# Graph network layer: sums of block pairs and of nodes turned by transposes instead of products with the identity

## The chip, the cores and the metric

The kernel runs on one core of a Trainium2 chip. Five engines of the core work on their own queues: TensorE (PE in the profile, its weight loads PEld), VectorE (DVE), ScalarE (ACT), GpSimd (POOL) and SyncE (SP, which here only issues transfers). The metric is the device time of one execution in microseconds. A kernel is timed in several runs and the median is taken. One further execution is recorded by the hardware profiler.

## The reference

A message-passing layer on a graph of 12,500 nodes and 400,000 edges, sorted by destination. Each node has 64 scalars and 32 vectors of three parts (160 numbers). Cut to its core:

```python
s, v = x[:, :64], x[:, 64:].reshape(n, 32, 3)
h_s = s @ lin1_ws * a / sqrt(64);  h_v = einsum('nci,cd->ndi', v, lin1_wv) * a / sqrt(32)
w1, w2, w3, w4, w5 = split(silu(edge_scalars @ fc_w1 / 8) @ fc_w2 / 8)   # 224 weights an edge
es, ev = h_s[src], h_v[src]                       # one row of 160 numbers for each edge
mid_s = concat(w1*es*e0, w4*einsum('eci,ei->ec', ev, e1)/sqrt(3))
mid_v = concat((w2*es)*e1, w3*ev*e0, w5*cross(ev, e1)/sqrt(2))
agg_s, agg_v = segment_sum(mid_s, dst)/4, segment_sum(mid_v, dst)/4
pre_s = sc_s + agg_s @ lin2_ws * a/sqrt(96);  pre_v = sc_v + einsum(agg_v, lin2_wv) * a/sqrt(128)
out = layernorm(x + concat(silu(pre_s[:, :64]), sigmoid(pre_s[:, 64:]) * pre_v))
```

All numbers are f32.

## The kernel before

**Tiles and blocks.** Edges go through in tiles of 128, one edge on each partition; 3,125 tiles. Three tiles are a block (1,042 blocks), and two blocks a pair (521 pairs), whose sums share one PSUM bank: one block on partitions 0 to 63, the other on 64 to 127. Since edges are sorted, the edges of a block reach few nodes; a window of `W` = 16 nodes from the block's first destination holds them (a loop at the end redoes the work if one does not). Four tiles are a step, and there are 782 steps.

**A step.** POOL issues four indirect transfers (`gather`, L471), each of which fetches 128 rows of `h_tab` into `hg`. TensorE makes the edges' 224 weights (`weights`, L546) from the hidden layer (`hidden`, L462, with ACT's activation L464) into `pw`. VectorE builds a one-hot of the destination within the window (L609), the products of weights and rows in `pr` (L556 and L564, 416 columns), and `sel` (L618), the one-hot times the four edge numbers. TensorE multiplies `sel` and `pr` into the bank `pa` (`add_tile`, L625): 64 rows for a block, which are four kinds (the scalar edge number and the three vector parts) times 16 nodes, and 416 columns.

**A pair's end.** When both blocks of a pair are summed, ACT copies `pa` to `sa` (`close`, L848). Some steps later `turned` brings channels onto the partitions: the 416 columns are taken as four groups of 128 (the last overlaps), and each is multiplied with those columns of the identity that hold the wanted kinds: the three vector kinds for groups 0 and 1, the scalar kind for groups 2 and 3. TensorE does this at L641, in the order of the pairs, and ACT copies the bank to `tt` (L644). There are 258 such calls for two pairs and five for one pair. When ten blocks are in `tt`, `second` multiplies them with the second weights (L654), ACT copies the result to `os` (L657), and VectorE adds each block's window to `acc` (`add`, L662).

**Nodes' ends.** When no open block can reach a group of 128-node tiles any more, `finish` turns their sums two tiles at a time: for each tile and each half (scalars, vectors) a product of the kept inputs with the `sc` weights (L709) and a product of `acc` with the identity (L711) are summed in one bank, `pp`. Then come the gates, the sum with `x` and the layer norm.

**The order.** All engines' orders are written out by hand (`manual_schedule`): every step puts its instructions on the queues in the order of the code. At step n TensorE gets weights(n), then at most a hidden layer, a turn or a second product (`spread_out`), and then the sums of step n-2. POOL's third gather of step n also waits for the weights of step n-2 (`behind`). `pw` has two buffers, `hg` five, `pr` and `sel` three. In every 66th step ACT's queue fetches the rows instead of POOL, one by one, spread over the steps before (L514).

Of the kernel before, what the change touches and what calls it, by code (L numbers as in the profile page):

```python
# [10 lines left out]
F32 = mybir.dt.float32  # L11
# [10 lines left out]
P = 128  # L22
S = 64
V = 32
V3 = 3 * V
# [6 lines left out]
W = 16  # L32
# [17 lines left out]
NPR = 2 * S + 3 * V3  # L50
ROWS = 4 * W
# [10 lines left out]
def gnn_kernel(  # L62
# [21 lines left out]
    nc = tc.nc  # L84
# [10 lines left out]
    consts = ctx.enter_context(tc.tile_pool(name="consts", bufs=1))  # L95
# [111 lines left out]

    ident = consts.tile([P, P], F32, name="ident")
    make_identity(nc, ident)
    iota_i = consts.tile([P, W], I32, name="iota_i")  # L210
    nc.gpsimd.iota(iota_i, pattern=[[1, W]], base=0, channel_multiplier=0)
    eps = consts.tile([P, 1], F32, name="eps")
# [19 lines left out]
    with tc.tile_pool(name="nodes", bufs=len(starts)) as nodes, tc.tile_pool(  # L232
        name="nodes_ps", bufs=6, space=PSUM
# [33 lines left out]
        for q in range(4):  # L267
            t0, s = divmod(q * QN, P)
            nc.gpsimd.dma_start(at_k[:P - s, q], attr[s:, t0:t0 + NQ])
            if s:  # L270
                m = min(NQ, NT - t0 - 1)
# [51 lines left out]
        for half in range(2):  # L323
            r = slice(half * S, (half + 1) * S)
# [14 lines left out]
        for c0, cn, xw, xz in loaded:  # L339
# [7 lines left out]
            n = min(cn, P)  # L347
# [7 lines left out]
            for u, c in enumerate(blocks):  # L355
# [8 lines left out]
                to = h_tab.rearrange("(q r) d -> r q d", q=4)[c0 + u * P:c0 + u * P + n]  # L364
# [39 lines left out]
    for to, part, pieces, w, r0, c0, by in maps:  # L404
        for k, piece in enumerate(pieces):
            four, at_p = divmod(PIECE[piece], 4)
            if four == 3:
                at_p = 3 - (len(PIECE) - 1) % 4 + at_p
            m = terms.setdefault((to, part, four), len(terms))
            at_r = at_p * V  # L410
            r = l2[at_r:at_r + V, m, c0:c0 + w.shape[1]]
# [16 lines left out]
    acc = sums.tile([V3, 2, NP], F32, name="acc")  # L428
# [199 lines left out]

    def turned(psum, sas, tt, b, n):

        pt = psum.tile([P, 8, 4, W], F32, name="pt", tag="misc")
        k = n * ROWS
        wanted = ident.rearrange("p (b k w) -> p k b w", b=2, k=4)[:k]
        for m, sa in enumerate(sas):
            plane = 0
            for four in range(4):
                c = min(four * P, NPR - P)
                of = slice(1, 4) if four < 2 else slice(0, 1)
                planes = slice(plane, plane + of.stop - of.start)
                plane = planes.stop  # L640
                nc.tensor.matmul(pt[:, planes, m * n:(m + 1) * n], sa[:k, c:c + P],  # L641
                                 wanted[:, of, :n], start=True, stop=True)
        n *= len(sas)
        nc.scalar.copy(tt[:, :, b:b + n], pt[:, :, :n])  # L644

    def second(pool, psum, tt, nb):
        po = psum.tile([V3, 2, NO, W], F32, name="po", tag="misc")
        for k, to in enumerate("sv"):
            of = [key for key in terms if key[0] == to]
            for n, (_, part, four) in enumerate(of):  # L650
                assert part and four < 2 or not part and four >= 2
                r = slice(P - V if four == 3 else 0, P)
                a = tt[r, four * 3 + part - 1 if part else 4 + four]
                nc.tensor.matmul(po[:, k, :nb], l2[r, terms[to, part, four]], a[:, :nb],  # L654
                                 start=(n == 0), stop=(n == len(of) - 1))
        os = pool.tile([V3, 2, NO, W], F32, name="os", bufs=1)
        nc.scalar.copy(os[:, :, :nb], po[:, :, :nb])  # L657
        return os
# [6 lines left out]
    def own_scalars_vectors(pool, c0, cn):  # L665

        xs = pool.tile([S, NF * P], F32, name="xs2")
        xv = pool.tile([V3, NF * P], F32, name="xv2")
        nc.sync.dma_start(xs[:, :cn], xs_t[:, c0:c0 + cn])
        nc.sync.dma_start(xv[:, :cn], xv_t[:, c0:c0 + cn])  # L670
        return xs, xv
# [8 lines left out]
    def finish(fin, psum, t0, nt, p, most=NF, pool=None):  # L680

        connect = pool is None and t0 + nt < tiles_of_nodes


        whole = nt if p == P else nt - 1
        xt = fin.tile([P, most, D], F32, name="xt") if pool is None else pool.tile([P, Q, D], F32, name="hg")
        if connect:
            xs, xv = own_scalars_vectors(fin, t0 * P, nt * P)
        held = []
        if whole < nt:  # L690
            nc.vector.memset(xt[:, whole], 0.0)
        parts = [(slice(t0 * P, (t0 + whole) * P), slice(0, whole), P)] if whole else []
        if whole < nt:
            parts.append((slice((t0 + whole) * P, (t0 + whole) * P + p), slice(whole, nt), p))
        for nodes_of, k, n in parts:
            nc.sync.dma_start(xt[:n, k], x[nodes_of, :].rearrange("(t p) d -> p t d", p=n))

        def turn(ks):
            if not held:
                held.extend(fin.tile([P, most, *shape], F32, name=name) for name, shape in (  # L700
                    ("g", [V3]), ("y", [D]), ("st", [6]), ("mv", [2]), ("rs", [])))
            g, y = held[:2]
            pp = psum.tile([P, 2, 2, V3], F32, name="pp", tag="misc")
            for k in ks:
                c = (t0 + k) * P
                for m in range(2):
                    if connect:
                        w, a = ((scs, xs), (scv, xv))[m]
                        nc.tensor.matmul(pp[:, k % 2, m], a[:, k * P:(k + 1) * P], w,  # L709
                                         start=True, stop=False)  # L710
                    nc.tensor.matmul(pp[:, k % 2, m], acc[:, m, c:c + P], ident[:V3, :V3],  # L711
                                     start=not connect, stop=True)
            for k in ks:
                nc.scalar.activation(g[:, k], pp[:, k % 2, 0], AF.Tanh, scale=half_at[:, t0 + k:t0 + k + 1])  # L714

            def gate():
                n = len(ks)
                k = slice(ks[0], ks[0] + n)
                nc.vector.scalar_tensor_tensor(y[:, k, :S], g[:, k, :S], 1.0, pp[:, :n, 0, :S],  # L719
                                               op0=OP.add, op1=OP.mult)  # L720
                for k in ks:
                    nc.vector.scalar_tensor_tensor(
                        y[:, k, S:].rearrange("p (c i) -> p i c", i=3),
                        g[:, k, None, S:].to_broadcast([P, 3, V]), 1.0,
                        pp[:, k % 2, 1].rearrange("p (i c) -> p i c", i=3),
                        op0=OP.add, op1=OP.mult)
                for k in ks:
                    nc.vector.scalar_tensor_tensor(y[:, k], y[:, k], half_at[:, t0 + k:t0 + k + 1],
                                                   xt[:, k], op0=OP.mult, op1=OP.add)

            return gate

        def moments():
            _, y, st, mv, _ = held
            for k in range(nt):
                nc.vector.bn_stats(st[:, k], y[:, k])
            for k in range(nt):
                nc.vector.bn_aggr(mv[:, k], st[:, k])

        def root():  # L740
            mv, rs = held[3:]
            nc.scalar.activation(rs[:, :nt], mv[:, :nt, 1], AF.Sqrt, bias=eps)

        def norm():
            _, y, _, mv, rs = held
            nc.vector.reciprocal(rs[:, :nt], rs[:, :nt])
            for k in range(nt):
                nc.vector.tensor_scalar(y[:, k], y[:, k], mv[:, k, 0:1], rs[:, k:k + 1],
                                        op0=OP.subtract, op1=OP.mult)
            for nodes_of, k, n in parts:  # L750
                nc.sync.dma_start(out[nodes_of, :].rearrange("(t p) d -> p t d", p=n), y[:n, k])

        return [lambda k=k: turn(range(k, min(nt, k + 2))) for k in range(0, nt, 2)] + [
            moments, root, norm]

# [9 lines left out]
    with tc.tile_pool(  # L765
        name="fin", bufs=1
    ) as fin, tc.tile_pool(
        name="mine", bufs=2
    ) as mine, tc.tile_pool(
        name="late", bufs=2  # L770
    ) as late, tc.tile_pool(name="edge", bufs=2) as edge, tc.tile_pool(
        name="deep", bufs=5
# [198 lines left out]
        with in_order:  # L971
# [74 lines left out]
            n = len(steps)  # L1046
# [29 lines left out]
        with tc.For_i(0, n_redo, 1):  # L1076
# [9 lines left out]
            with tc.For_i(0, n_again, 1) as g, tc.For_i(0, GT, 1) as k:  # L1086
# [7 lines left out]
                to = loads.tile([P, 1], I32, name="to1", bufs=1)  # L1094
# [15 lines left out]
                r = edge.tile([P, 1], F32, name="r", bufs=1)  # L1110
# [10 lines left out]
                with tc.For_i(first, last + 1, W) as base:  # L1121
# [5 lines left out]
                    sa = late.tile([P, NPR], F32, name="sa", bufs=3)  # L1127
                    nc.scalar.copy(sa[:ROWS], pa[:ROWS, :NPR])
                    tt = late.tile([P, 8, NO, W], F32, name="tt", bufs=1)
# [55 lines left out]
```

## Time and profile before

| | us |
|---|---|
| median of three runs | 4739.37 (4736.33 to 4754.99) |
| the profiled execution, its own time | 4726.69 |
| its span, first to last instruction | 4724.9 |
| busy in the span: PE / POOL / DVE / ACT | 4059.0 / 2944.0 / 2368.9 / 849.7 |

In rows of the profile, a group is a line, an engine, an operation, the tiles written and read, and a count; then busy time and the mean duration of one in ns, and the engine's idle time just before, with what ended it. In rows of equal stretches, a time stands for each engine (PE, PEld, DVE, ACT, POOL) with a count in brackets, then the clock granted to TensorE as a share of full speed, the transfers' share and GB/s. Durations of matmul passes overlap, so the pace of a group is read from one start to the next.

### The profile page before, as it was taken

Reading aid. Unit: us, or ns where it says so; the run is one execution under the profiler, and the core shown is the slowest. Engines: PE = TensorE matmul, PEld = TensorE weight load, DVE = VectorE, ACT = ScalarE, POOL = GpSimd, SP = SyncE. Lnnn points to the kernel's source line nnn. Section 1 sums busy time; section 2 is a strip of 40 time slices with the busy share of each in tenths; the row PEclk is TensorE's granted clock in tenths of the full one; section 3 lists DMA queues with packets and bytes.
Section 4 is the critical chain, followed back from the end, with each engine's and each line's share of the span. In section 5 each row is a group of like instructions: output and inputs, shape, how many; then the busy total and the mean of one; then the engine's idle time right before and its main releaser. Section 6 shows DMA issues by size and latency. Waiting matters only on the chain.

```text
span 4724.9 us, 69481 instructions
## 1 busy us (share of the span) xinstructions
PE 4059.0 (86%) x19977; PEld 2169.9 (46%) x19977; DVE 2368.9 (50%) x6421; ACT 849.7 (18%) x1828; POOL 2944.0 (62%) x3128
## 2 busy tenths in 40 slices
PE   6888888888888888888888888888888888888887
PEld 4444444444444444444444444444444444444444
DVE  5544544545544454455455445445445445544454
ACT  2111111111111111111121111111111111111112
POOL 6666666666666666666666666666666666666663
PEclk8888988988988889898998888888889888898898
DMA  6333333333333333333333333333333333333331
GB/s 212 87 77 79 91 86 79 91 78 86 94 77 86 78 94 86 77 94 83 80 93 85 84 89 87 84 86 79 91 88 79 91 81 87 91 80 88 78 92 50
DMA packets 253104, 413.30 MB, mean 87 GB/s; under 512 B 89304, under 2 KB 177153, under 8 KB 252581
## 3 DMA queue, kind: packets, MB, share of 16 engines
q0 software_dynamic: 150848, 263.03, 21.2%
q1 hardware_dynamic: 90004, 141.98, 12.6%
q10 hardware_dynamic: 11858, 3.76, 0.4%
q8 instruction: 159, 2.61, 0.2%
q14 instruction: 235, 1.93, 0.1%
HBM read 392.51 MB, written 16.00 MB: 86 GB/s over the span
## 4 chain that ended last, share of the span: by engine, by line
PE 52%; issue 15%; ACTq 9%; another core or an unknown queue 8%; DVE 8%; POOL 5%; DMA 2%; ACT 1%; DVEq 0%; SPq 0%; POOLq 0%
PE pa L625 18%; PE pw L546 12%; PE misc L641 8%; ACTq L514 7%; PE misc L462 6%; POOL hg L471 5%; PE misc L654 5%; DVE pr L564 4%; ACTq L507 2%; PE misc L711 1%; DMA hg<-h_tab,idx 1%; PE misc L709 1%; DVE sel L618 1%; DVE pr L556 1%
## 5 line engine op out<-in xcount | busy, mean ns | idle before, releaser
L471 POOL DMA_INDIRECT hg<-h_tab,idx x3081 | 2913.4, 946 | 1724.2 <-issue 792.5
L625 PE MATMUL pa<-pr,sel 128*64 128x416 f32 x6250 | 1564.8, 594 | 122.4 <-issue 120.5
L546 PE MATMUL pw<-w,hid 64*128 64x224 f32 x6250 | 988.1, 407 | 276.8 <-issue 178.9
L609 DVE TENSOR_TENSOR pw<-rel,iota 128x64 f32<-128x64 int16 x782 | 179.2, 229 | 1986.6 <-remote 1121.5
L564 DVE TENSOR_TENSOR pr<-pw,hg 128x384 f32<-128x384 f32 x2313 | 1137.6, 547 | 0.0
L546 PEld LDWEIGHTS pw<-w,hid 64*128 64x128 f32 x6250 | 626.1, 204 | 942.7 <-issue 653.7
L625 PEld LDWEIGHTS pa<-pr,sel 128*64 128x64 f32 x6250 | 445.8, 151 | 962.0 <-issue 921.4
L641 PE MATMUL misc<-ident,sa 128*128 128x96 f32 (+1 forms) x4168 | 600.2, 296 | 80.2 <-issue 76.9
L641 PEld LDWEIGHTS misc<-ident,sa 128*128 128x128 f32 x4168 | 559.2, 211 | 172.1 <-issue 154.5
L556 DVE TENSOR_TENSOR pr<-pw,hg 128x512 f32<-128x512 f32 x771 | 532.7, 691 | 38.5 <-DVE pw L609 5.1
L462 PE MATMUL misc<-es,w 128*128 128x512 f32 (+1 forms) x784 | 479.7, 695 | 43.4 <-DVE rel L424 20.0
L464 ACT ACTIVATE hid<-misc 128x512 f32<-128x512 f32 x392 | 233.1, 595 | 1092.7 <-issue 565.1
L644 ACT COPY tt<-misc 128x512 f32<-128x512 f32 (+1 forms) x263 | 152.8, 581 | 1434.0 <-remote 784.6
L654 PE MATMUL misc<-tt,l 128*96 128x256 f32 (+5 forms) x1496 | 371.8, 395 | 14.8 <-issue 14.2
L618 DVE TENSOR_TENSOR sel<-pw,eas 128x256 f32<-128x256 f32 x782 | 324.1, 415 | 0.1
L848 ACT COPY sa<-pa 128x416 f32<-128x416 f32 x521 | 262.2, 503 | 283.0 <-remote 83.8
L654 PEld LDWEIGHTS misc<-tt,l 128*96 128x96 f32 (+1 forms) x1496 | 232.0, 169 | 146.5 <-issue 81.2
L462 PEld LDWEIGHTS misc<-es,w 128*128 128x128 f32 x784 | 129.1, 205 | 174.1 <-issue 135.1
L662 DVE TENSOR_TENSOR acc<-acc,os 96x32 f32 x1042 | 192.1, 184 | 25.5 <-ACT os L657 7.0
L711 PE MATMUL misc<-ident,acc 96*128 96x96 f32 x392 | 115.0, 393 | 95.6 <-DVE acc L662 62.2
L719 DVE SCALAR_TENSOR_TENSOR y<-g,misc 128x128 f32<-128x128 f32 x49 | 14.1, 287 | 265.8 <-ACT g L714 75.4
L711 PEld LDWEIGHTS misc<-ident,acc 96*128 96x128 f32 x392 | 86.5, 276 | 112.3 <-DVE acc L662 66.9
(93 smaller groups left out, 726.2 us busy)
## 6 DMA issues: line engine op xcount, KB each, us to landing
es<-in_es_t_dram SPq DMA_DIRECT2D x258, 384.0 KB
hq<-h_tab ACTq DMA_DIRECT2D x5632, 0.6 KB
hg<-h_tab,idx POOLq DMA_INDIRECT x3081
h_tab<-ht POOLq DMA_DIRECT2D x24, 320.0 KB
xt<-in_x_dram SPq DMA_DIRECT2D x23, 320.0 KB
out_dram<-y SPq DMA_DIRECT2D x23, 320.0 KB
xv<-in_xv_t_dram SPq DMA_DIRECT2D x23, 192.0 KB
eat<-in_ea_dram SPq DMA_DIRECT2D x41, 96.0 KB
```

The costliest lines, as they stand in the source:

```text
L462: nc.tensor.matmul(ph[:k, c], w1[:k, :k], es[:k, t0 * P + c0 * P:t0 * P + c1 * P], start=True, stop=True)
L471: got = nc.gpsimd.indirect_dma_start(out=hg[:, t, :], out_offset=None, in_=h_tab, in_offset=bass.IndirectOffsetOnAxis(ap=i, axis=0))
L514: row = queue.dma_start(flat_hq[p:p + 1, t * row_bytes:(t + 1) * row_bytes], by_bytes[ds(v, row_bytes)][None])
L546: weighed.append(nc.tensor.matmul(pw[:, t, :NWT], hid[r, c * P:(c + 1) * P], w2[r], start=True, stop=True).ins.name)
L556: nc.vector.tensor_mul(two, pw[:, :n, :2 * S].rearrange("p t (k c) -> p t k c", k=2), hg[:, :n, None, :S].to_broadcast([P, n, 2, S]))
L564: nc.vector.tensor_mul(pr[:, :n, first:first + V3].rearrange("p t (i c) -> p t i c", i=3), pw[:, :n, None, 2 * S + k * V:2 * S + (k + 1) * ...
L618: nc.vector.tensor_mul(sel[:, :n], oh[:, :, None, :].to_broadcast([P, n, 4, W]), by_slot(tiles[0][0])[:, u:u + n, :, None].to_broadcast([P ...
L625: summed.append(nc.tensor.matmul(pa[half * ROWS:(half + 1) * ROWS, :NPR], sel[:, t].rearrange("p k w -> p (k w)"), pr, start=start, stop=s ...
L641: nc.tensor.matmul(pt[:, planes, m * n:(m + 1) * n], sa[:k, c:c + P], wanted[:, of, :n], start=True, stop=True)
L654: nc.tensor.matmul(po[:, k, :nb], l2[r, terms[to, part, four]], a[:, :nb], start=(n == 0), stop=(n == len(of) - 1))
L711: nc.tensor.matmul(pp[:, k % 2, m], acc[:, m, c:c + P], ident[:V3, :V3], start=not connect, stop=True)
L848: nc.scalar.copy(sa, pas.pop(j)[:, :NPR])
```

## The change

`turned` uses TensorE's transpose with a moving operand that is a permutation, instead of a product with some columns of the identity. A transpose has to write all four kinds (128 columns), so each also writes kinds that are not wanted, and the order of the writes is such that a later one overwrites them. Two permutations are used: the identity with its columns ordered by kind (`by_first`, scalar kind first) and a new constant, `first_last`, with the scalar kind last (`by_last`), which VectorE fills at the start. For two pairs, seven writes are transposes and one is still a product (the scalar kind of the second pair's third group, 32 columns). The second pair now comes first. The planes of `tt` stand in another order, so `second` reads others, and ACT's copy brings the pairs together. In `finish` the sums of nodes are turned by transposes as well, which start the bank; the product of the kept inputs follows and is added.

```diff
+    first_last = consts.tile([P, P], F32, name="first_last")
+    by_kind = ident.rearrange("p (b k w) -> p k b w", b=2, k=4)
+    ordered = first_last.rearrange("p (k b w) -> p k b w", b=2, k=4)
+    nc.vector.tensor_copy(ordered[:, :3], by_kind[:, 1:])
+    nc.vector.tensor_copy(ordered[:, 3:], by_kind[:, :1])
...
     def turned(psum, sas, tt, b, n):
-        pt = psum.tile([P, 8, 4, W], F32, name="pt", tag="misc")
-        k = n * ROWS
-        wanted = ident.rearrange("p (b k w) -> p k b w", b=2, k=4)[:k]
-        for m, sa in enumerate(sas):
-            plane = 0
-            for four in range(4):
-                c = min(four * P, NPR - P)
-                of = slice(1, 4) if four < 2 else slice(0, 1)
-                planes = slice(plane, plane + of.stop - of.start)
-                plane = planes.stop
-                nc.tensor.matmul(pt[:, planes, m * n:(m + 1) * n], sa[:k, c:c + P],
-                                 wanted[:, of, :n], start=True, stop=True)
-        n *= len(sas)
-        nc.scalar.copy(tt[:, :, b:b + n], pt[:, :, :n])
+        pt = psum.tile([P, 512], F32, name="pt", tag="misc")
+        k, w = n * ROWS, n * W
+        fours = {four: min(four * P, NPR - P) for four in range(4)}
+        by_first = ident.rearrange("p (b k w) -> p k b w", b=2, k=4)[:k, :, :n]
+        by_last = first_last.rearrange("p (k b w) -> p k b w", b=2, k=4)[:k, :, :n]
+        writes = [(0, 2, 0, by_first), (0, 3, 1, by_first), (0, 0, 2, by_last), (0, 1, 5, by_last)]
+        if len(sas) == 2:
+            writes = [(1, 1, 12, by_first), (1, 0, 9, by_first), (1, 3, 6, by_last), *writes,
+                      (1, 2, 8, by_first[:, :1])]
+        for m, four, at_p, moving in writes:
+            of = sas[m][:k, fours[four]:fours[four] + P]
+            kinds = moving.shape[1]
+            to = pt[:, at_p * w:(at_p + kinds) * w]
+            nc.tensor.matmul(to.rearrange("p (k b w) -> p k b w", k=kinds, b=n), of, moving,
+                             start=True, stop=True, is_transpose=kinds == 4)
+        m = len(sas)
+        nc.scalar.copy(
+            tt[:, :, b:b + n * m].rearrange("c f (m b) w -> c m f (b w)", m=m),
+            pt[:, :8 * w * m].rearrange("c (m f x) -> c m f x", m=m, f=8))
...
-                a = tt[r, four * 3 + part - 1 if part else 4 + four]
+                a = tt[r, 2 + four * 3 + part - 1 if part else four - 2]
...
                 for m in range(2):
+                    nc.tensor.matmul(pp[:, k % 2, m], acc[:, m, c:c + P], ident[:V3, :V3],
+                                     start=True, stop=not connect, is_transpose=True)
                     if connect:
                         w, a = ((scs, xs), (scv, xv))[m]
                         nc.tensor.matmul(pp[:, k % 2, m], a[:, k * P:(k + 1) * P], w,
-                                         start=True, stop=False)
-                    nc.tensor.matmul(pp[:, k % 2, m], acc[:, m, c:c + P], ident[:V3, :V3],
-                                     start=not connect, stop=True)
+                                         start=False, stop=True)
```

The first place is a call of `turned` for two pairs on TensorE, between the weights of one step and the sums two steps before it (`misc` is the bank it writes, `sa` the pairs' sums; a product stands here as one row, though the profile shows two passes of it). Before:

```order
L546 MATMUL pw_509<-w_92,hid 128x224 x4
L641 MATMUL misc_512<-ident,sa 128x3x32 x2
L641 MATMUL misc_512<-ident,sa 128x32 x2
L641 MATMUL misc_512<-ident,sa 128x3x32 x2
L641 MATMUL misc_512<-ident,sa 128x32 x2
L625 MATMUL pa_511<-pr,sel 64x416 x4
```

and with the change:

```order
L551 MATMUL pw_511<-w_95,hid 128x224 x4
L649 MATMUL misc_516<-ident,sa 128x128 x2
L649 MATMUL misc_516<-first_last,sa 128x128
L649 MATMUL misc_516<-ident,sa 128x128 x2
L649 MATMUL misc_516<-first_last,sa 128x128 x2
L649 MATMUL misc_516<-ident,sa 128x32
L630 MATMUL pa_514<-pr,sel 64x416 x4
```

There are still eight calls at the same place; seven of them stream 128 columns instead of 96 or 32, and the last is the product that is left.

The second place is one turn of two node tiles on TensorE, after the weights of a step (`acc` holds the nodes' sums, `scs` and `scv` are the weights of the kept inputs `xs` and `xv`). Before:

```order
L546 MATMUL pw_508<-w_92,hid 128x224 x4
L709 MATMUL misc_513<-scs,xs_1475 128x96
L711 MATMUL misc_513<-ident,acc 128x96
L709 MATMUL misc_513<-scv,xv_1476 128x96
L711 MATMUL misc_513<-ident,acc 128x96
```

and with the change:

```order
L551 MATMUL pw_511<-w_95,hid 128x224 x4
L717 MATMUL misc_516<-ident,acc 128x96
L721 MATMUL misc_516<-scs,xs_1478 128x96
L717 MATMUL misc_516<-ident,acc 128x96
L721 MATMUL misc_516<-scv,xv_1479 128x96
```

What reads `acc` now stands first, ahead of the product of the kept inputs.

## The prediction

> **What bounds the kernel now.** I read the page first, then the chain of waits, and then, because the two did not fit the gather engine's rows, POOL's own timeline and the busy time of equal stretches.
>
> ```profile
> PE 4059.0 (86%) x19977; PEld 2169.9 (46%) x19977; DVE 2368.9 (50%) x6421; ACT 849.7 (18%) x1828; POOL 2944.0 (62%) x3128
> PE 52%; issue 15%; ACTq 9%; another core or an unknown queue 8%; DVE 8%; POOL 5%; DMA 2%; ACT 1%; DVEq 0%; SPq 0%; POOLq 0%
> L471 POOL DMA_INDIRECT hg<-h_tab,idx x3081 | 2913.4, 946 | 1724.2 <-issue 792.5
> L556 DVE TENSOR_TENSOR pr<-pw,hg 128x512 f32<-128x512 f32 x771 | 532.7, 691 | 38.5 <-DVE pw L609 5.1
> L641 PE MATMUL misc<-ident,sa 128*128 128x96 f32 (+1 forms) x4168 | 600.2, 296 | 80.2 <-issue 76.9
> L711 PE MATMUL misc<-ident,acc 96*128 96x96 f32 x392 | 115.0, 393 | 95.6 <-DVE acc L662 62.2
> ```
>
> On these rows TensorE looks like the bound: busy 86%, half of the chain. POOL looks idle for a third of the time. Its timeline says otherwise:
>
> ```profile
> 2215.57 0.94 POOL L471 DMA_INDIRECT hg<-h_tab,idx  x1 [2.24 <-remote]
> 2216.82 0.94 POOL L471 DMA_INDIRECT hg<-h_tab,idx  x1 [0.30 <-issue]
> ...
> 2224.31 0.95 POOL L471 DMA_INDIRECT hg<-h_tab,idx  x1 [0.30 <-issue]
> 2227.51 0.95 POOL L471 DMA_INDIRECT hg<-h_tab,idx  x1 [2.25 <-PE pw L546]
> ```
>
> Gathers start every 1.25 us, eight in a burst, and then comes a pause of about 2.25 us. A burst with its pause takes 2227.51 - 2215.57 = 11.94 us, that is two steps. If TensorE set this length, it would follow TensorE's work. The next rows are such bursts, each from its first gather to the next burst's first; the bracket behind PE counts its matmul passes.
>
> ```profile
> 2215.57:2227.51 11.94, 9.94 (x37) 5.79 (x34) 3.53 (x9) 2.17 (x6) 7.56 (x8) 0.57 0.31 83
> 2239.64:2251.65 12.01, 10.90 (x63) 6.90 (x60) 6.59 (x17) 4.43 (x7) 7.56 (x8) 1.00 0.31 85
> 2263.77:2275.69 11.92, 8.74 (x46) 4.63 (x45) 5.78 (x16) 2.12 (x9) 7.57 (x9) 0.93 0.21 57
> 2275.69:2287.55 11.86, 11.86 (x49) 6.81 (x49) 5.78 (x16) 1.68 (x4) 7.53 (x8) 0.64 0.21 56
> 2299.39:2311.24 11.85, 9.81 (x47) 5.06 (x44) 5.58 (x15) 1.96 (x4) 7.58 (x9) 1.00 0.22 58
> 2371.37:2383.39 12.02, 10.57 (x64) 5.62 (x61) 6.86 (x24) 1.53 (x3) 7.60 (x9) 0.99 0.63 150
> ```
>
> From 37 to 64 passes, and with a granted clock (the number after POOL) from 0.57 to 1.00, the length stays between 11.85 and 12.02 us. The only thing that is the same in all of them is the eight gathers (a ninth is one that straddles an edge). So a gather with its share of the pause costs about 11.9/8 = 1.49 us, and this sets the pace. Over the whole run:
>
> ```profile
> 500.00:1000.00 500.00, 432.79 (x2119) 227.37 (x2118) 249.98 (x684) 89.40 (x195) 310.13 (x329) 0.89 0.34 85
> ...
> 4000.00:4500.00 500.00, 431.44 (x2147) 229.11 (x2149) 254.43 (x694) 87.77 (x194) 315.44 (x334) 0.90 0.34 85
> ```
>
> The eight stretches of 500 us from 500 to 4500 hold 329 to 336 gathers each, 2667 together: 1.50 us per gather. At 1.4875 they would take 3967 us. So only 33 us of 4000 (38 us over the run) are left for anything that stretches a burst, TensorE among it. What makes the pause I cannot name: of two equal pauses above the profile puts one down to an unknown releaser and one to the weights, pw.
>
> **The change, part by part.** *Turning the sums of block pairs.* A product of two f32 operands is two passes in the trace (521 pairs with four products each are the 4168 passes of L641). A call for two pairs is 16 passes:
>
> ```profile
> 2470.12 1.97 PE L641 MATMUL misc<-ident,sa 128*128 128x96 f32 x16
> 2472.03 1.62 PE L625 MATMUL pa<-pr,sel 128*64 128x416 f32 x8
> ```
>
> From start to next start that is 1.91 us, 0.119 us a pass. The new call has seven transposes and one product: nine passes, if a transpose is one. There is one transpose in the old kernel:
>
> ```profile
> 207.67 0.37 PE L791 MATMUL misc<-ident,far 128*1 128x128 f32 x1 [5.21 <-DVE far L788]
> 207.97 1.86 PE L546 MATMUL pw<-w,hid 64*128 64x224 f32 x8
> ```
>
> It is one record for one call, with 128 columns streamed as in the new calls; so the change does what it says. Its price beside neighbours is not shown. Below, the 0.119 us of the product passes, which load the same 128 columns of weights; above, the 0.30 us to the next start here, behind a wait and with one loaded column. I take 0.119, since the passes replaced have the same shape of load and stand in the same rows. With 258 calls for two pairs and five for one (258 x 16 + 5 x 8 = 4168) 4168 passes become 258 x 9 + 5 x 4 = 2342; 1826 x 0.119 = 217 us of TensorE time go. At the upper price a call takes 7 x 0.30 + 2 x 0.119 = 2.34 us, 0.43 us more than now, 111 us of TensorE time over 258 calls.
>
> The Trainium skill, TensorE: Matmul & The Clock Gate, Part 4 (PE-mode transpose), gives about 275 ns for a 128x128 transpose in one kernel's context; by it a call would take 7 x 0.275 + 0.24 = 2.16 us, and TensorE's time would grow by an estimated 65 us instead of shrinking by 217. The lone record here, 0.37 us with 0.30 us to the next start, is no evidence against that.
>
> *The order inside a call.* The second pair's sum now comes first. Before, a late second copy held up only the second half:
>
> ```profile
> 2062.31 0.19 PEld L641 LDWEIGHTS misc<-ident,sa 128*128 128x128 f32 x1 [0.32 <-issue]
> ...
> 2065.14 1.24 PEld L641 LDWEIGHTS misc<-ident,sa 128*128 128x128 f32 x8 [0.22 <-ACT sa L848]
> ```
>
> Here the whole call would wait until 2065.14, and behind it on TensorE the sums and the weights of the next steps, for which VectorE and the gathers wait. Few calls have this, so between nothing and the eight passes' 0.95 us per call; I take nothing, covered by the slack below.
>
> *Nodes' turns.* 392 passes of L711 become 196, and the product of kept inputs moves from ahead of the transpose to behind it:
>
> ```profile
> 2003.92 0.35 PE L709 MATMUL misc<-scs,xs 64*128 64x96 f32 x2
> 2007.81 0.74 PE L711 MATMUL misc<-ident,acc 96*128 96x96 f32 x2 [3.53 <-DVE pr L564]
> ...
> 2011.53 0.96 PE L625 MATMUL pa<-pr,sel 128*64 128x416 f32 x2
> ```
>
> Behind the wait stand 14 passes in 3.72 us, 0.27 us each; now there are 12, so 0.53 us less, and for the 47 turns that have this product 25 us of TensorE time.
>
> *The rest.* ACT's copy moves the same 512 elements. Two small copies at the start, under 0.7 us together by L556's 0.69 us for 512 columns, lie on VectorE ahead of the first work of the program; I count 0.3 us. The planes' new places change addresses alone.
>
> **The sum.** 242 us of TensorE time go, 0.62 us per two steps. Its cover is the pause of the bursts: the six rows above leave it idle 0 to 3.2 us in 11.9, and length does not follow passes, so within the steady bursts I count nothing. Where the cut is on the path:
>
> ```profile
> 4668.89 4.22 PE L641 MATMUL misc<-ident,sa 128*128 128x96 f32 x24
> 4673.04 1.86 PE L546 MATMUL pw<-w,hid 64*128 64x224 f32 x8
> ...
> 4707.83 3.73 PE L711 MATMUL misc<-ident,acc 96*128 96x96 f32 x16 [1.28 <-DVE acc L662]
> ...
> 4675.19 0.95 POOL L471 DMA_INDIRECT hg<-h_tab,idx  x1 [8.48 <-PE pw L546]
> ```
>
> At the end POOL waits 8.48 us for weights that stand behind 24 turning passes, and after the last gather TensorE is the chain. Eleven of these 24 go (11 x 0.176 = 1.9 us), 19 of the 40 after them (2.3 us), and eight of the last 16 (1.9 us): 6 us. Of the 38 us that stretch bursts I give the cut 14; bounds 0 and 38. Together 4726.7 (the profiled execution: span 4724.9 and 1.8 around it) - 20 = 4706.7. The median of the runs shown is 12.7 above it: 4719, rounded to 4718; by the bounds and the 6 us, 4695 to 4733, and its own range is 4690 to 4735.
>
> **Rivals.** *TensorE is the bound, as its 86% and the chain say.* Then up to 242 us come off: 4497; by the chain's 67% for PE and issue 162 us, 4577; middle 4540. Against it stand the rows from 37 to 64 passes. It would need the pause to be TensorE's lateness after all, shortened by being earlier.
>
> *Bursts grow longer.* A few bursts are of twelve:
>
> ```profile
> 2474.40:2491.92 17.52, 10.97 (x59) 5.52 (x57) 7.83 (x23) 2.42 (x8) 11.34 (x12) 0.82 0.22 59
> ```
>
> That is 1.46 us per gather, 0.03 less. If weights that are done earlier let most bursts run on, 3081 x 0.03 = 92 us come off: 4645. For it: the gather after the pause does wait for weights. Against: these weights wait for VectorE first, which is not changed.
>
> *Slower: the clock.* The granted clock falls after a stretch in which TensorE does little (the second and third row; the first is the mean of the run):
>
> ```profile
> core 0: 4724.9 us, clock 0.883
> ...
> 2003.90:2007.30 3.40, 0.37 (x4) 0.20 (x2) 2.51 (x6) 1.10 (x2) 1.89 (x2) 1.00 0.19 51
> 2007.30:2010.70 3.40, 2.89 (x11) 2.55 (x12) 1.25 (x5) 0.00 (x0) 2.60 (x3) 0.57 0.29 76
> ```
>
> If transposes do not count as work, each call is such a gap, and one beside another wait tips the clock. TensorE's 86% is 10.2 us of 11.9; less 0.62 it is 9.6 at the mean clock of 0.88 (first row). It fills the 11.9 us once the mean clock is under 0.88 x 9.6/11.9 = 0.71, and from there it sets the time: at 0.69 a burst takes 12.25 us, 0.35 x 391 = 137 us more, 4860; at 0.70 12.07 us, 66 us more, 4785. Against: a call of 1 us is a third of the 3.4 us nearly empty here, and the row of clock 0.57 above took 11.94 us too. The Trainium skill's Part 4 named above states that transposes do not count as busy in the same way; the one transpose of this trace cannot show it.
>
> **How the numbers follow.** Gathers set the time, small gain: 0.62. TensorE the bound: 0.14. Longer bursts: 0.09. Clock: 0.15. About 0.5% (24 us) is what a measurement of this kernel can tell from no change; of the first case I put 0.39 within it and 0.23 beyond. Faster is 0.23 + 0.14 + 0.09 = 0.46, same 0.39, slower 0.15. The range takes in the upper end of the TensorE case and the clock case down to a mean clock of 0.70: 4570 to 4780, which leaves out some 0.10 below and 0.08 above.
>
> **What would show it.** Right: the turning rows fall to 2342 passes, PE's busy share falls by four or five points, and the stretches still hold 329 to 336 gathers per 500 us with pauses near 2.2 us. A transpose's price: the time from a call's start to the next group, 1.07 us here, over 1.9 if it runs alone. Wrong: over 345 gathers per 500 us (TensorE was the bound, or bursts of twelve are common), or a mean clock under 0.71.

## The result and the profile after

| | before | changed |
|---|---|---|
| median of four runs, us | 4740.15 (4736.33 to 4754.99) | 4696.17 (4686.28 to 4703.92) |
| the profiled execution, us | 4726.69 | 4696.53 |

The ratio is 0.990, with a 95% interval from 0.9872 to 0.9929: 44 us faster, twice the 21 us that were forecast, on the side that was forecast and within the range.

From the changed kernel's page, the busy times, the chain of waits by engine, and the groups of the gathers, of the turning writes and of the nodes' transposes:

```profile
PE 3740.4 (80%) x17955; PEld 1866.6 (40%) x17955; DVE 2369.9 (50%) x6423; ACT 852.4 (18%) x1828; POOL 2943.9 (63%) x3128
PE 41%; DVE 15%; issue 15%; another core or an unknown queue 15%; POOL 7%; ACTq 5%; DMA 2%; ACT 1%; DVEq 0%; SPq 0%; POOLq 0%
L476 POOL DMA_INDIRECT hg<-h_tab,idx x3081 | 2913.4, 946 | 1695.3 <-issue 813.6
L649 PE MATMUL misc<-ident,sa 128*128 128x128 f32 (+1 forms) x1558 | 328.3, 301 | 230.7 <-issue 140.4
L649 PE MATMUL misc<-first_last,sa 128*128 128x128 f32 x784 | 199.3, 311 | 12.9 <-issue 12.6
L717 PE MATMUL misc<-ident,acc 96*128 96x96 f32 x196 | 68.0, 353 | 166.7 <-DVE pw L614 118.0
```

TensorE has 2022 passes fewer (19977 - 17955), as the change says: 1558 + 784 = 2342 turning passes are left of 4168, and 196 of the nodes' 392. Its busy time fell by 319 us and by six points of the span, the time of the program by 30 us (of these two executions). POOL's busy time is the same to 0.1 us, and its idle time ahead of gathers fell from 1724.2 to 1695.3 us: 28.9 us, nearly the whole difference. So what these two executions gained was gained in POOL's pauses. In the rows of equal stretches the same is seen as more gathers in 500 us (the number behind POOL):

```profile
500.00:1000.00 500.00, 404.77 (x1914) 196.78 (x1912) 252.81 (x692) 90.80 (x196) 314.09 (x333) 0.88 0.34 86
...
4000.00:4500.00 500.00, 403.80 (x1931) 199.46 (x1931) 252.96 (x692) 91.08 (x204) 315.57 (x334) 0.88 0.35 87
```

The eight stretches from 500 to 4500 hold 333 to 338 gathers (329 to 336 before), 2688 together instead of 2667. 21 gathers at 1.49 us are 31 us.

One call of the turning, with a granted clock of 1.00, from the timeline of TensorE (start, length, line, count):

```profile
4658.09 0.44 PE L649 MATMUL misc<-ident,sa 128*128 128x128 f32 x2
4658.36 0.27 PE L649 MATMUL misc<-first_last,sa 128*128 128x128 f32 x1
4658.47 0.38 PE L649 MATMUL misc<-ident,sa 128*128 128x128 f32 x2
4658.69 0.38 PE L649 MATMUL misc<-first_last,sa 128*128 128x128 f32 x2
4658.91 0.31 PE L649 MATMUL misc<-ident,sa 128*128 128x32 f32 x2
4659.15 1.03 PE L551 MATMUL pw<-w,hid 64*128 64x224 f32 x8
```

Nine passes in 4659.15 - 4658.09 = 1.06 us; 1.07 were forecast. The lone transpose of the second row lasts 0.27 us, and the next starts 0.11 us after it: one transpose is long, but here they follow each other at 0.11 us, close to the 0.119 us of the product passes that they replace. The prediction's upper price, 0.30 us from the one transpose of before, was read where the granted clock was 0.50.

### The profile page after: what moved, and what is told of

The parts are those of the page before. It is cut to its first block, busy times and chain, and to the rows that moved or that the text cites. A ratio compares the mean times of both kernels' runs of the same rounds, so it can differ in the third digit from the quotient of the medians.

```text
span 4694.7 us, 65476 instructions
## 1 busy us (share of the span) xinstructions
PE 3740.4 (80%) x17955; PEld 1866.6 (40%) x17955; DVE 2369.9 (50%) x6423; ACT 852.4 (18%) x1828; POOL 2943.9 (63%) x3128
## 3 DMA queue, kind: packets, MB, share of 16 engines
q0 software_dynamic: 150848, 263.03, 21.6%
q1 hardware_dynamic: 90004, 141.98, 12.7%
q8 instruction: 143, 2.34, 0.2%
## 4 chain that ended last, share of the span: by engine, by line
PE 41%; DVE 15%; issue 15%; another core or an unknown queue 15%; POOL 7%; ACTq 5%; DMA 2%; ACT 1%; DVEq 0%; SPq 0%; POOLq 0%
PE pa L630 14%; PE pw L551 10%; DVE pr L569 9%; POOL hg L476 7%; PE misc L664 5%; PE misc L467 4%; PE misc L649 4%; ACTq L519 4%; DVE sel L623 2%; PE misc L721 2%; DVE pr L561 2%; DMA hg<-h_tab,idx 1%; DVE pw L614 1%; PE misc L717 1%
## 5 line engine op out<-in xcount | busy, mean ns | idle before, releaser
L476 POOL DMA_INDIRECT hg<-h_tab,idx x3081 | 2913.4, 946 | 1695.3 <-issue 813.6
L630 PE MATMUL pa<-pr,sel 128*64 128x416 f32 x6250 | 1533.6, 590 | 96.8 <-issue 91.5
L551 PE MATMUL pw<-w,hid 64*128 64x224 f32 x6250 | 943.0, 398 | 318.5 <-issue 176.3
L551 PEld LDWEIGHTS pw<-w,hid 64*128 64x128 f32 x6250 | 601.8, 199 | 948.3 <-issue 600.9
L649 PE MATMUL misc<-ident,sa 128*128 128x128 f32 (+1 forms) x1558 | 328.3, 301 | 230.7 <-issue 140.4
L467 PE MATMUL misc<-es,w 128*128 128x512 f32 (+1 forms) x784 | 467.0, 674 | 52.4 <-issue 25.3
L664 PE MATMUL misc<-tt,l 128*96 128x256 f32 (+5 forms) x1496 | 391.3, 407 | 38.6 <-issue 35.2
L649 PEld LDWEIGHTS misc<-ident,sa 128*128 128x128 f32 x1558 | 231.6, 181 | 328.1 <-issue 217.2
L649 PE MATMUL misc<-first_last,sa 128*128 128x128 f32 x784 | 199.3, 311 | 12.9 <-issue 12.6
L717 PE MATMUL misc<-ident,acc 96*128 96x96 f32 x196 | 68.0, 353 | 166.7 <-DVE pw L614 118.0
L467 PEld LDWEIGHTS misc<-es,w 128*128 128x128 f32 x784 | 123.7, 196 | 181.5 <-issue 161.8
L649 PEld LDWEIGHTS misc<-first_last,sa 128*128 128x128 f32 x784 | 120.1, 162 | 16.4 <-issue 16.0
```

Of the source, the lines that this page charges most:

```text
L467: nc.tensor.matmul(ph[:k, c], w1[:k, :k], es[:k, t0 * P + c0 * P:t0 * P + c1 * P], start=True, stop=True)
L476: got = nc.gpsimd.indirect_dma_start(out=hg[:, t, :], out_offset=None, in_=h_tab, in_offset=bass.IndirectOffsetOnAxis(ap=i, axis=0))
L551: weighed.append(nc.tensor.matmul(pw[:, t, :NWT], hid[r, c * P:(c + 1) * P], w2[r], start=True, stop=True).ins.name)
L630: summed.append(nc.tensor.matmul(pa[half * ROWS:(half + 1) * ROWS, :NPR], sel[:, t].rearrange("p k w -> p (k w)"), pr, start=start, stop=s ...
L649: nc.tensor.matmul(to.rearrange("p (k b w) -> p k b w", k=kinds, b=n), of, moving, start=True, stop=True, is_transpose=kinds == 4)
```

## The experiments

The twelve runs were made on four chips, each beside the kernel before on the same chip. On the first three chips the kernel before takes 3956 us, not 4740, and in the traces from there gathers hardly ever pause; on the fourth, which had only the last run, it takes 4774 us. All expectations below were written with one of these two pictures in mind, and the ratio to the kernel before is what compares runs of different chips.

**The change again.** No edit.

> The changed kernel itself, beside the kernel before on the same chip. The four runs so far showed the kernel before at 3956.6 us instead of 4740, with gathers starting every 1.25 us without any pause. If this chip shows no pauses either: gathers set the time at 3081 x 1.25 = 3851 us plus start and end, so the change is worth only what lies after the last gather, 4 to 8 us, 3949 to 3953 us. If it shows pauses: 4690 to 4700 us beside 4740, 30 to 50 us less, as first measured.

Measured: 3950.24 us beside 3955.88, ratio 0.9985 (0.9975 to 0.9995). The timeline of POOL, here and in the first measurement of the changed kernel, shows what differs. First this run, 16 gathers in a row:

```profile
2207.34 0.95 POOL L476 DMA_INDIRECT hg<-h_tab,idx  x1 [0.30 <-issue]
...
2216.11 0.95 POOL L476 DMA_INDIRECT hg<-h_tab,idx  x1 [0.30 <-issue]
2217.36 0.95 POOL L476 DMA_INDIRECT hg<-h_tab,idx  x1 [0.30 <-issue]
...
2226.11 0.95 POOL L476 DMA_INDIRECT hg<-h_tab,idx  x1 [0.30 <-issue]
```

and then the first measurement:

```profile
2209.68 0.94 POOL L476 DMA_INDIRECT hg<-h_tab,idx  x1 [0.30 <-issue]
2213.00 0.94 POOL L476 DMA_INDIRECT hg<-h_tab,idx  x1 [2.38 <-PE pw L551]
...
2221.75 0.95 POOL L476 DMA_INDIRECT hg<-h_tab,idx  x1 [0.30 <-issue]
2224.79 0.94 POOL L476 DMA_INDIRECT hg<-h_tab,idx  x1 [2.09 <-PE pw L551]
```

A gather takes 0.95 us and starts 1.25 us after the one before in both. Only the pause of some 2.2 us after eight is missing here: a gather starts over 1.6 us after the one before it three times in this run and 413 times in the first measurement. Without pauses the program is the gathers' time, 3081 x 1.25 = 3851 us, with a start and an end, and 2022 passes less of TensorE are worth 6 us.

**One part alone.** The first run keeps the changed `turned` and has `finish` as before:

```diff
-                    nc.tensor.matmul(pp[:, k % 2, m], acc[:, m, c:c + P], ident[:V3, :V3],
-                                     start=True, stop=not connect, is_transpose=True)
                     if connect:
                         w, a = ((scs, xs), (scv, xv))[m]
                         nc.tensor.matmul(pp[:, k % 2, m], a[:, k * P:(k + 1) * P], w,
-                                         start=False, stop=True)
+                                         start=True, stop=False)
+                    nc.tensor.matmul(pp[:, k % 2, m], acc[:, m, c:c + P], ident[:V3, :V3],
+                                     start=not connect, stop=True)
```

The second is the kernel before with these lines the other way round, the transpose first.

> Only the turning of block pairs is changed; the nodes' turns are as before. It removes 1826 of the 2022 passes. Theory (gathers set the time, TensorE's cut shows only where a burst was stretched): the gain of the whole change, 44 us, splits about as the TensorE time does, so some 30 us of it come here, 4705 to 4715 us. Rival (TensorE sets the time): about two thirds of it too, but then the doubled writes of the fourth run must cost far more than 50 us.

> Only the nodes' turns are changed; block pairs are turned as before. It removes 196 passes and lets the reader of acc stand first. Theory: 10 to 20 us less than before, 4720 to 4730 us, since turns of nodes stand in stretched bursts (8 of the 26 worst of before). If the order mattered more than the passes, all 44 us could be here: 4696 us.

Measured: 0.9986 (0.9977 to 0.9995) and 1.0005 (0.9996 to 1.0014). Both figures in us were written for a chip with pauses and missed by the whole of its difference. The split itself is clear where there are no pauses: the block pairs bring all of the 6 us, the nodes nothing that can be told from zero. How the 44 us of the first measurement divide was not measured.

**The order of the two pairs.** The sums that were copied first are turned first:

```diff
-            turned(misc_ps, [sa for _, sa in js], tts[0], len(turns), 2)
-            for j, _ in js:
+            turned(misc_ps, [sa for _, sa in js[::-1]], tts[0], len(turns), 2)
+            for j, _ in js[::-1]:
```

> The whole change, but the pair whose sums were copied first is turned first. In the changed kernel turning waits 192 us in all for ACT's copy sa (89 before products, 103 before weight loads). Theory: three of nine writes run ahead of that wait, at most 0.33 us of 258 calls, 85 us of TensorE time, of which a tenth shows: 0 to 10 us less than the changed kernel, 4686 to 4696 us. Rival (TensorE sets the time): 40 us or more less.

Measured: 0.9987 (0.9978 to 0.9996), the change's own 0.9985 within the interval. The order is worth nothing here.

**Twice the work.** Every write of a call is issued twice:

```diff
-        for m, four, at_p, moving in writes:
+        for m, four, at_p, moving in [w for w in writes for _ in range(2)]:
```

> The whole change, and every write of a block pairs' call is issued twice in a row: 2342 more passes, about 0.115 us each, 270 us more work for TensorE. Theory (gathers set the time): the change took 378 us of TensorE's time away and gained 44, so 0.12 us per us: about 30 us more than the changed kernel, 4710 to 4740 us. Rival (TensorE sets the time): by the 56% that PE and issue have of the chain 150 us more, 4845 us; by its whole time 270 us, 4965 us.

The 378 us in this expectation stand in no page; the busy time fell by 319. Measured: 0.9996 (0.9987 to 1.0005). The same 500 us of the change and of the doubled writes, the first row the change's:

```profile
1000.00:1500.00 500.00, 434.62 (x2294) 219.84 (x2292) 300.63 (x826) 106.81 (x232) 378.08 (x401) 0.92 0.44 103
```

```profile
1000.00:1500.00 500.00, 460.27 (x2581) 252.05 (x2580) 301.50 (x827) 106.78 (x232) 377.80 (x399) 0.93 0.44 103
```

287 passes more in 500 us, 26 us more of TensorE's busy time, and two gathers fewer. Over the run 2342 passes cost 0.0011 x 3956 = 4 us. That is far under the 150 to 270 us of the theory that TensorE sets the time, which falls with this on a chip without pauses. It is also under the 30 us of the gathers' theory, which took its rate from the first measurement.

**The gathers' number.** With all rows of a kind fetched by POOL, 44 gathers more:

```diff
-OWN = 66
+OWN = 100000
```

> The changed kernel without steps whose rows ACT's queue fetches: POOL issues 44 more gathers, 3125 in all. Theory (gathers set the time): 44 x 1.25 = 55 us more than the changed kernel without pauses, 44 x 1.49 = 66 us more with them. Rival (TensorE or VectorE sets the time): no change, or a few us less since 5632 row transfers go.

Measured: 1.0113 (1.0096 to 1.013), 4000.69 us, 50 us over the change on the same chip: 1.15 us a gather. On this chip the gathers' number sets the time.

**The wait for the weights.** Without the wait of the third gather:

```diff
-                    deep, [index(t) for t, _, _ in tiles], {2: weighed_by[n - 2] if n >= 6 else None})
+                    deep, [index(t) for t, _, _ in tiles], None)
```

> The changed kernel without the wait of each step's third gather for the weights of two steps before; a gather then waits for its buffer alone. Theory (a gather takes 1.25 us of POOL whatever it waits for): no change without pauses, 3945 to 3960 us; with pauses no change either, if they come from buffers that are late, 4680 to 4710 us. Rival (the wait itself makes the pause): with pauses 4000 to 4400 us, from 3081 x 1.25 = 3851 us up to TensorE's time; without pauses no difference between the two.

Measured: 3947.07 us, 0.9977 (0.9967 to 0.9986). Without pauses the wait costs some 3 us, and the intervals of the two ratios overlap. Whether it makes the pauses on a chip that has them stays open: the run fell on a chip without.

**Gathers that wait for TensorE.** To make gathers wait for TensorE on a chip without pauses, the third gather waits for the weights of one step before instead of two, in both kernels:

```diff
-{2: weighed_by[n - 2] if n >= 6 else None}
+{2: weighed_by[n - 1] if n >= 6 else None}
```

> The kernel before, with the third gather of a step waiting for the weights of one step before instead of two. This makes gathers wait for TensorE, as they did in the first measurement, and is read together with the next run. Without pauses in the kernel before: bursts now end at a wait for weights, so slower than 3956 us, somewhere between 4050 and 4700 us. If weights are always long done when they are waited for: no change.

> The changed kernel with the same tighter wait. Theory (378 us of TensorE's time are worth little where gathers run back to back, and more where a gather waits for weights): the difference to the run with the kernel before is well over the 6 us found without pauses: 30 to 100 us less, as 44 us in the first measurement. Rival (the larger gain of the first measurement has nothing to do with the gathers' wait for weights): again 4 to 8 us less.

Measured on one chip: 4052.45 us, ratio 1.0252 (1.0235 to 1.0269), and with the change 4007.01 us, ratio 1.0126 (1.011 to 1.0143). The change is worth 45 us here, 1.1%, beside 6 us with the looser wait. POOL's waits for weights (total us, times, longest), first in the kernel before, then with the change, then in the change with the looser wait:

```profile
POOL hg L471 <- PE pw L546: 128.0, 87, 6.2
```

```profile
POOL hg L476 <- PE pw L551: 87.5, 79, 7.7
```

```profile
POOL hg L476 <- PE pw L551: 22.4, 48, 4.1
```

128.0 - 87.5 = 40 of the 45 us are this one wait. So the same cut of TensorE's work is worth some seven times as much where gathers wait for what TensorE makes, though the gathers set the pace in all three. It does not copy the first measurement: 60 pauses stand in the trace of the kernel before with the tighter wait, 442 in that of the first measurement.

**Fewer gathers, more of ACT's rows.** Every 44th step's rows are fetched by ACT's queue, three a slot:

```diff
-OWN = 66
-SLOTS = (2,2,2,2)
+OWN = 44
+SLOTS = (3,3,3,3)
```

> The changed kernel with every 44th step's rows fetched by ACT's queue instead of every 66th, three rows a slot instead of two: 17 such steps instead of 11, 24 gathers fewer. Theory (gathers set the time): 24 x 1.25 = 30 us less than the changed kernel without pauses, 24 x 1.49 = 36 us less with them. Rival: no change, or slower, if ACT with half as many transfers more becomes late with its copies.

Measured: 4159.62 us, 1.0478 (1.0407 to 1.0549). The rival came true. The chain of waits by engine of this run:

```profile
ACTq 52%; PE 16%; issue 12%; DVE 3%; ACT 2%; DMA 1%; POOL 1%; SPq 0%; DVEq 0%; POOLq 0%
ACTq L519 40%; ACTq L512 12%; PE pa L630 5%; PE misc L664 5%; PE pw L551 3%; PE misc L649 2%; DVE pr L569 1%; PE misc L467 1%; ACT sa L858 1%; POOL hg L476 1%; ACT eas L597 0%; DMA hg<-h_tab,idx 0%; DVE sel L623 0%; ACT tt L652 0%; ACT hid 
```

ACT issues twelve rows a step, and its own work (the activation for the weights, the copies of sums) stands behind them. Fetching rows isn't free: each costs its queue's engine an issue (L519) and a share of loading the places (L512).

**Rows on two queues.** The rows go to ACT's and SP's queues in turn:

```diff
-OWN = 66
-TURNS = "A"
-SLOTS = (2,2,2,2)
+OWN = 33
+TURNS = "AS"
+SLOTS = (4,4,4,4)
```

> The changed kernel with every 33rd step's rows fetched by queues other than POOL's, one row from ACT's queue and one from SP's in turn, four a slot: ACT still issues two a slot, as in the changed kernel, and SP the other two. 12 more such steps, 48 gathers fewer. Theory (gathers set the time, and the run with every 44th step was slower because ACT's queue alone issued three a slot): 48 x 1.25 = 60 us less than the changed kernel without pauses, 3890 us; 48 x 1.49 = 72 us less with them. Rival (SP's queue, which also loads the edges' data, becomes late, or fetching rows delays what else the DMA engines move): slower than the changed kernel.

Measured: 3893.15 us, 0.9843 (0.9826 to 0.9859), the fastest of all kernels on these chips: 0.9985 - 0.9843 = 1.4% or 56 us under the change, 1.17 us for each of the 48 gathers.

One step further, with three of five rows on SP:

```diff
-OWN = 33
-TURNS = "AS"
-SLOTS = (4,4,4,4)
+OWN = 27
+TURNS = "ASASS"
+SLOTS = (5,5,5,5)
```

> As the run with every 33rd step's rows on ACT's and SP's queues, but every 27th: of five rows a slot two go to ACT's queue, as in the changed kernel, and three to SP's. 28 such steps instead of 11, 68 gathers fewer than the changed kernel. Theory (gathers still set the time): 68 x 1.25 = 85 us less than the changed kernel without pauses, 3865 us; with pauses 68 x 1.49 = 101 us less. Rival (TensorE, busy 86% of the run with every 33rd step, or SP's queue, twelve rows a step, is now the bound): no faster than that run's 3893 us.

Measured: 5949.04 us beside 4774.43, ratio 1.2445 (1.241 to 1.248), on a chip on which gathers pause. From the chain of waits and the list of waits:

```profile
SPq 47%; issue 31%; PE 11%; DMA 4%; POOL 3%; DVE 2%; another core or an unknown queue 1%; ACTq 0%; ACT 0%; DVEq 0%; POOLq 0%
...
PE misc L467 <- DMA es<-in_es_t_dram: 1645.8, 113, 27.9
...
POOL hg L476 <- PE pw L551: 1328.6, 180, 24.9
```

SP's queue is the bound: the edges' data `es` come behind the rows in it, the hidden layer (L467) waits for them up to 27.9 us, and the gathers for the weights behind it. Whether twelve rows a step would be too much for SP on the other chips, or eight a step too much on this one, can't be told from one run: the fastest kernel above is shown only for chips without pauses.

## Why the prediction held, and where it was too small

**What bounds the kernel.** The step "this sets the pace", of the gathers, holds on chips without pauses, where it was tested: 44 more cost 50 us, 48 fewer bring 56, 2342 more passes cost 4. The price of 1.49 us with its share of a pause fits the first measurement; without pauses it is 1.25 us. The prediction could not name what makes the pause. The two traces of the first measurement show where the pauses stand and which of them are TensorE's, as told under the sum; what makes the others is still open.

**The turning's price.** 0.119 us a pass was right (1.06 us a call for 1.07). The upper bound of 0.30 us, from the lone transpose, would have made the call 2.34 us. The Trainium skill, TensorE: Matmul & The Clock Gate, Part 4 (PE-mode transpose), gives about 275 ns in one kernel's context, next to a figure for bf16; the f32 trace here agrees with it as the length of one, 0.27 us, and not as the pace of several, 0.11 us.

**The order and the nodes.** Nothing for the order: shown, where there are no pauses. The nodes' 196 passes went, and without pauses they brought nothing.

**The sum.** The traces show 30.2 us less, where 20 were forecast. Two terms were mis-sized.

"Of the 38 us that stretch bursts I give the cut 14" was too little. From the times of all gathers and all weights in the two traces: the stretch from the first gather to the end of the last one went from 4633.6 to 4604.1 us, 29.5 us less, and 28 of these are pauses. A pause is counted here where a gather starts over 1.6 us after the one before, and its length is what is over 1.25 us. There were 442 pauses with 779 us, and with the change 413 with 751 us. Nearly all, 433 and 402 of them, stand before the third gather of a step, the one that also waits for the weights of two steps before. Yet most of them are not TensorE's lateness. Where the weights really are late, the gather starts 0.28 us after the end of their last pass, as at the long wait of POOL near the end, in the changed kernel:

```profile
4645.68 1.03 PE L551 MATMUL pw<-w,hid 64*128 64x224 f32 x8
```

```profile
4646.99 0.95 POOL L476 DMA_INDIRECT hg<-h_tab,idx  x1 [8.25 <-PE pw L551]
```

The gather at 2224.79 that was shown with the first run also has a wait for weights in its bracket. But the weights that it has to wait for had ended at 2219.39, 5.4 us earlier:

```profile
2218.36 1.03 PE L551 MATMUL pw<-w,hid 64*128 64x224 f32 x8
```

Pauses that end within 0.5 us of these weights were 21 with 63.7 us, and with the change 12 with 39.4 us: 24 us less. The other pauses before a third gather went from 412 with 704 us to 390 with 699 us, though the weights had been done for a median of 4.9 and 6.7 us. So "within the steady bursts I count nothing" held to some 5 us, and what was too small is the term for gathers that really wait. A late weight may stand where another pause would have come, so this is a split of the pauses that are there, not a price of each.

"6 us" at the end was too much. Of it, 1.9 us were meant for POOL's long wait, which went from 8.48 to 8.25 us, and 4.2 us for what follows the last gather; from that gather's end to the end of the span 39.2 us became 38.3. The 19 turning passes there brought what was forecast, 2.4 us up to the start of the last nodes' turn (2.3 forecast). The last 16 passes brought nothing, since behind them VectorE waits for a write of `y` to the output, before and with the change:

```profile
4711.47 0.29 DVE L719 SCALAR_TENSOR_TENSOR y<-g,misc 128x128 f32<-128x128 f32 x1 [2.10 <-DMA out_dram<-y]
```

```profile
4681.27 0.29 DVE L729 SCALAR_TENSOR_TENSOR y<-g,misc 128x128 f32<-128x128 f32 x1 [3.58 <-DMA out_dram<-y]
```

These starts lie 3.6 and 5.1 us behind the start of the last nodes' turn (4707.83 and 4676.15), so 1.5 of the 2.4 us were lost again. POOL's long wait stayed with another cause. What stood ahead of its weights on TensorE, in the changed kernel:

```profile
4636.19 0.39 PE L717 MATMUL misc<-ident,acc 96*128 96x96 f32 x1 [8.53 <-DVE pw L614]
...
4639.57 3.04 PE L630 MATMUL pa<-pr,sel 128*64 128x416 f32 x8
```

TensorE idles 8.53 us ahead of a nodes' turn, until VectorE is done, and shorter turning calls behind that turn shorten POOL's wait little.

The other 14 of the medians' 44 us are in no trace: the profiled execution of before lay 13.5 us under its median, that of the changed kernel 0.4 above its own. "12.7 above" was carried over to the changed kernel, and did not hold.

**Rivals.** TensorE as the bound: wrong without pauses (doubled writes), and wrong in the first measurement, where it would have brought 162 to 242 us and where most pauses end long after the weights. Longer bursts: they did grow, those of four went from 109 to 60 and those of ten or more from 9 to 21. But the pauses that are not for weights cost 704 us before and 699 after, so this brought little. The clock: the mean granted clock was 0.883 and is 0.885:

```profile
core 0: 4694.7 us, clock 0.885
```

It did not tip. On the chips without pauses all runs lie close together: before 0.927 to 0.932, changed 0.919 to 0.924, doubled writes 0.942 to 0.946. In these runs the clock was higher where TensorE had more to do, and seven of the eight writes that were doubled in a call are transposes. The Trainium skill's Part 4 named above states that transposes do not count as busy in the same way; the doubled writes speak against it here, since their clock lies even above that of the kernel before, which turned block pairs by products alone. The eighth write, a product, was doubled too, so this is not shown for transposes alone.

**Why 44 there and 6 here.** With the tighter wait the change is worth 45 us on a chip without pauses, of which 40 is the gathers' wait for weights. In the traces of the first measurement 24 of the 28 us that the pauses lost are the same wait. With the looser wait and no pauses such a wait is nearly absent: 3 gathers have one in the change's run, 8 us in all, and there the cut brought 6 us. So the 30 us that the two traces differ by are in the main this wait. The figures are from one execution of each kernel. What stays open is what makes the other pauses, 412 before and 390 with the change, and why they come on some chips alone. That they stand before the one gather that waits for weights makes that wait a suspect; the kernel without it would tell on a chip with pauses, and it ran only on one without.

## What to carry to other kernels

An engine that is busy 86% and has half of the chain can still not be the bound: find the engine whose instructions follow each other at a fixed distance, and see whether the length of a stretch follows its count or the other's work. What a cut on another engine is worth is then set by the waits between the two: 6 us where the pacing engine hardly ever waited, 45 where it did, for the same cut. A wait that the profile puts down to an engine is that engine's lateness only if its work ended just before the wait did: in the kernel before 101 waits of POOL carry the weights' name, and 21 pauses ended just behind them. A gain measured on one chip is a gain for that chip's waits; a second one belongs to the measurement.

## What the runs showed of the hardware

The same kernel takes 3956 us on three chips and 4740 or 4774 elsewhere, with the same duration of each gather (946 and 947 ns). The gathers' packets were not slower where there were pauses. The share of the POOL queue in the 16 engines' span, first measurement of the changed kernel and then its run without pauses:

```profile
q0 software_dynamic: 150848, 263.03, 21.6%
```

```profile
q0 software_dynamic: 150848, 263.03, 27.3%
```

21.6% of 4694.7 us are 1014 us, 27.3% of 3952.4 are 1079. So slower packets are not what makes the pauses; whether something else on a transfer's way is late is not shown.
